# Layer 0 of a four-layer convolution stack: PSUM as one tile, four-bank results, copies of 768 columns

## The chip, the cores and the metric

The kernel runs on one core of a Trainium2 chip. Its time is the device time of one execution in microseconds (us), as a median over runs. A profile of one further execution shows what each engine did: TensorE (PE, with its weight loads, PEld), VectorE (DVE), ScalarE (ACT), GpSimd (POOL), and SyncE (SP), which issues DMAs.

## The reference, cut to what matters

The input is x with 4 images of 64 channels of 256 x 256, float32. Four layers follow one another; each adds to x a function of the group-normalised x. Only layer 0 is touched by the change:

```python
x = jnp.einsum('bchw,oc->bohw', x, w_in)            # 64 -> 384 channels, per pixel
xf = jnp.fft.rfft2(patches of 8 x 8) * fft_filter   # per channel, then back
x = depthwise 3 x 3 convolution of that
x1, x2 = jnp.split(x, 2, axis=1)
x = jax.nn.gelu(x1, approximate=False) * x2
return jnp.einsum('bchw,oc->bohw', x, w_out)        # 192 -> 64 channels
```

The filter on a patch and the depthwise convolution together are one linear map from the 64 pixels of a patch (and its neighbours) to 64 pixels, one for each of the 384 channels. Layer 1 is a 3 x 3 convolution, layer 2 a masked choice between two 1 x 1 convolutions, layer 3 a product in the Fourier domain.

## The kernel before, in words

Layer 0 cuts each image into rows of patches (32 rows, 32 patches each) and takes them in blocks of 11 rows: three blocks an image, 12 in all. For each block it loops four times (`kb`) over 48 channels of each kind, in two stages.

*Expansion* (`expand`, lines 459 to 490). One step takes half a normalised pair of patch rows from `xns`: 16 patches for each of two rows (index `s`; one row lies on partitions 0 to 63, the other on 64 to 127; at an image's edge the two halves hold the two halves of one row). The pixels are the stationary operand, `w_in` the moving one, so that a result has pixels of a patch on the partitions and channels along the columns. With `pairs` true (line 470) a stationary holds two neighbouring patches, 128 columns, and 16 matmuls make a step; otherwise (line 476) each patch is a stationary of its own and goes to the half of the partitions that suits the copies; that takes 32 matmuls. `pairs` is true for `kb` 0 and for the first six steps of the other passes (line 797).

The results of a step go to two PSUM tiles of two banks, one per `s`. PSUM is four such tiles, taken in turn by `banks` (line 278), for every purpose in layer 0. ScalarE copies the tile of `s` = 0 to the SBUF array `u`, VectorE that of `s` = 1: four copies each of 64 partitions x 384 columns when paired (line 486), three each otherwise (one of 128 partitions and two of 64; lines 488 to 490). `u` has a place for each patch of the block: on partitions 0 to 63 even patches at E1 and odd ones at O1, on partitions 64 to 127 odd ones at O2 and even ones at E2.

*Patch map* (`own` and `beside`, lines 514 to 550). For each group of two times two channels, 8 matmuls with the patch's own pixels (line 523) and 24 with those of its neighbours (line 539) accumulate in two tiles of `banks`; ScalarE takes the gelu of one bank (line 546), VectorE multiplies by the other (line 547), and POOL stores the result `h` to DRAM (line 550). Between groups, `unit` runs a part of the projection of the block before: `project` reads `g` back, multiplies by `w_out` (lines 632 and 639), and VectorE adds the result to x (lines 648 to 653).

The order on TensorE, VectorE, ScalarE and SP is as the code is written (`tc.manual_schedule`), so each engine goes through its instructions in program order. The framework sets the semaphores: it records which parts of which tiles an instruction reads and writes, and lets a later instruction wait for an earlier one that it conflicts with.

A block has 11 or 12 steps of expansion for each `kb` (`steps_of`, line 450): 32 stretches of 11 and 16 of 12, 544 steps in all.

Of the kernel before, what the change touches and what calls it, by code (L numbers as in the profile page):

```python
# [10 lines left out]
F32 = mybir.dt.float32  # L11
# [107 lines left out]
class _Net:  # L119
# [152 lines left out]
    def _layer0(self, ctx, dst):  # L272
        tc, nc, a, B, H, W = self.tc, self.nc, self.a, self.B, self.H, self.W
        pool = lambda name, bufs, **k: ctx.enter_context(tc.tile_pool(name=name, bufs=bufs, **k))
        pp = pool("l0p", 1, space=PSUM)
        turn = count()

        def banks(name):

            return pp.tile([128, 2, 512], F32, tag=f"p{next(turn) % 4}", name=name)  # L280

        self.small = lambda name: banks(name)[:, 0, :]
        P = PATCH
# [3 lines left out]
        CW = 2 * HC  # L287
# [3 lines left out]
        PB = HID // 4  # L291
        NR = 11
        L = CW * NR
        NG = PB // 4
        halves = [slice(0, C), slice(C, 128)]
# [121 lines left out]
        def load_x(part, p_x=p_x):  # L417
            b, i, k = part
            x0[part] = t = p_x.tile([128, 4, W], F32, tag="x", name=f"x0_{b}_{i}_{k}")
            for s in range(2):  # L420
                if k < 2:
                    nc.sync.dma_start(t[halves[s]], a["x"][b, :, P * (i + s) + 4 * k : P * (i + s) + 4 * k + 4, :])
                else:
                    nc.sync.dma_start(
                        t[halves[s]].rearrange("p r w -> p (r w)").rearrange("p (r w) -> p r w", r=P),
                        a["x"][b, :, P * i : P * i + P, s * HW2 : (s + 1) * HW2],
                    )

        def normalize_x(part, pool=False):
            b, i, k = part  # L430
            x = x0.pop(part).rearrange("p r w -> p (r w)")
            if k == 2:
                xns[b, i] = p_x1.tile([128, HW2 // P, P, P], F32, tag="x1", name=f"xn_{b}_{i}")
            elif k == 0:
                xns[b, i] = p_xn.tile([128, W // P, P, P], F32, tag="xn", name=f"xn_{b}_{i}")
            to = xns[b, i].rearrange("p m r w -> p r m w")
            if k < 2:
                to = to[:, 4 * k : 4 * k + 4]
            x = x.rearrange("p (r m w) -> p r m w", r=P if k == 2 else 4, w=P)
            if pool:  # L440
                nc.gpsimd.tensor_scalar(to, x, self.r[0][:, b : b + 1], self.nb[0][:, b : b + 1], ALU.mult, ALU.add)
            else:
                self.normalize(to, x, 0, b)
# [4 lines left out]
        E1, O1, O2, E2 = 0, HC, 1, HC  # L448

        def steps_of(p):  # L450

            b, i0 = blocks[p]
            one = lambda t: [(b, i0 + t, 0, [(t, 0), (t, 1)])] if 0 <= i0 + t < NP else []
            out = one(0)
            for t in range(1, NR, 2):
                out += [(b, i0 + t, q, [(t, q), (t + 1, q)]) for q in range(2)]
            return out + one(NR)

        def expand(p, kb, step, pairs):

            b, i, q, to = step
            ps = [banks(f"psu_{p}_{kb}_{i}_{q}_{s}") for s in range(2)]
            xn = xns[b, i][:, 16 * q : 16 * q + 16]
            lo, hi = halves
            for k in range(2):
                for m in range(4):
                    n, at = 2 * (4 * k + m), slice(2 * PB * m, 2 * PB * (m + 1))
                    for s in range(2):
                        if pairs:
                            nc.tensor.matmul(  # L470
                                ps[s][:, k, at], xn[halves[s], n : n + 2].rearrange("p n r w -> p (n r w)"),
                                win[halves[s], kb, 0 : 2 * PB], start=True, stop=True,
                            )
                            continue
                        for odd in range(2):
                            nc.tensor.matmul(  # L476
                                ps[s][halves[1 - odd], k, at], xn[halves[s], n + odd].rearrange("p r w -> p (r w)"),
                                win[halves[s], kb, PB * (1 - odd) : PB * (3 - odd)], start=True, stop=True,
                            )
            at = lambda h, o: u[h, :, o : o + 8].rearrange("p c (s m) -> p c s m", s=2)  # L480
            for s, copy in enumerate((nc.scalar.copy, nc.vector.tensor_copy)):
                o0 = to[s][0] * CW + 8 * to[s][1]
                v = ps[s][:, :, 0 : 8 * PB].rearrange("p s (m c) -> p c s m", m=4)
                if pairs:
                    for h, o, k, c in ((lo, O1, lo, 0), (hi, O2, lo, PB), (lo, E1 + 1, hi, 0), (hi, E2 + 1, hi, PB)):
                        copy(at(h, o0 + o), v[k, c : c + PB])  # L486
                    continue
                copy(at(slice(0, 128), o0 + 1), v[:, 0:PB])
                copy(at(hi, o0 + E2 + 1), v[lo, PB:])
                copy(at(lo, o0 + O1), v[hi, PB:])  # L490

        def load_w(j):

# [110 lines left out]
        def load_half(p, r, half):  # L604
            if 0 <= p < NB and r < P:
                if half == 0 and (p, r) not in rts:
                    load_r(p, r)
                load_g(p, r, half)
# [73 lines left out]
        with ordered:  # L682
# [38 lines left out]
            u = None  # L721
            ctx_u = ExitStack()
            u = ctx_u.enter_context(tc.tile_pool(name="l0u", bufs=1))
            u = u.tile([128, PB, (NR + 1) * CW + 2], F32, name="u")
            sources = []
            rows_u = u[:, :, 0 : (NR + 1) * CW].rearrange("p c (t w) -> p c t w", w=CW)
            lo, hi = halves
# [9 lines left out]
            for p in range(NB + 1):  # L737
# [24 lines left out]
                b, i0 = blocks[p]  # L762
                fresh = parts_of(p + 1) if p + 1 < NB else []
                steps = steps_of(p)
# [6 lines left out]
                def load_next(kb):  # L771
                    if kb == 3:
                        load_rows(2)
                    elif nk:
                        loaded.append(nk.pop(0))
                        load_stats(b + 1, loaded[-1])
# [10 lines left out]
                for kb in range(4):  # L787
                    for t in range(NR + 1):
                        if p == 0 and kb == 0:
                            if t == 1:  # L790
                                for part in first_parts[len(kept) :]:
                                    load_x(part)
                            for n in range(4) if t == 0 else range(t + 3, t + 4):
                                if n < len(first_parts):
                                    normalize_x(first_parts[n], pool=n % 2 == 1)
                        if t < len(steps):
                            expand(p, kb, steps[t], kb == 0 or t < (NR + 1) // 2)
                        if t in (0, 4) and first:
                            load_half(*first.pop(0))
                        if t == NR:  # L800
                            load_w(p * (HID // 8) + NG * kb // 2 + 3)
                            load_next(kb)
                    if p == 0 and kb == 0:
                        clear_sides()
                        ctx_f.close()
                        p_1, p_6 = (pool(n, 2, side="right") for n in ("l0g1", "l0g6"))
                        sources.append([p_1, p_6, pool("l0r", 2, side="right")])
                    for g in range(0, NG, 2):
                        if g > 0:
                            load_w(p * (HID // 8) + (NG * kb + g) // 2 + 3)  # L810
                        if g in (0, 2, 6, 8):
                            unit()
                        if g < 6 and kb < 3:
                            load_next(kb)
                        if kb == 3 and g == 0:
                            assert not self.norms
                            normalize_rows(3)
                        for k in range(2):
                            own(p, kb, g + k)
                        for k in range(2):  # L820
                            beside(p, kb, g + k)
                        if g < NG - 2 or kb == 2:
                            self.next_norms()
                        if kb == 3:
                            normalize_rows(2)
                            if p == NB - 1 and g < 2 * (NR // 2):
                                load_r(p, g // 2)
                            continue
                        if loaded:
                            next_stats(b + 1, loaded.pop(0))  # L830
                        if kb == 2 and g == NG - 2:
                            load_rows(2)
# [730 lines left out]
```

## Time and profile before

| | |
|---|---|
| median of 3 runs | 6347.42 us (6346.17 to 6354.44) |
| the profiled execution | 6345.01 us, span 6343.0 us |
| mean granted TensorE clock | 0.960 |
| PE busy | 5965.4 us (94% of the span) |
| weight loads | 3328.8 us (52%) |
| DVE busy | 4315.4 us (68%) |
| ACT busy | 3274.7 us (52%) |
| POOL busy | 1054.2 us (17%) |
| layer 0 | from the start to about 3790 us |

Busy times are sums over the whole span, so they mix stages with different limits; a line of a cost group gives the source line, engine, operation, what it writes and reads with shapes, the count, busy time and mean length of one, and then the engine's idle time just before those instructions with what ended it. Line numbers are those of the kernel before.

### The profile page before, as it was taken

The numbers are of one execution on the slowest core, as the hardware profiler recorded it, in microseconds if no ns is written. First come the engines' busy times: TensorE is split into PE (matmuls) and PEld (weight loads), VectorE is DVE, ScalarE is ACT, GpSimd is POOL, SyncE is SP. The second block draws the span as 40 slices with busy tenths as digits, with TensorE's granted clock in tenths as the row PEclk, the third lists the DMA queues.
The fourth block names the chain that finished last, engine by engine and source line by source line (L and its number), as shares of the span: only waits on it lengthen the run. The fifth ranks groups of instructions, "written<-read, shape, count | busy, mean of one in ns | idle before, by whom it ended". The sixth has DMA issues, their size and how long they took to land.

```text
span 6343.0 us, 233229 instructions
## 1 busy us (share of the span) xinstructions
PE 5965.4 (94%) x104150; PEld 3328.8 (52%) x104150; DVE 4315.4 (68%) x6003; ACT 3274.7 (52%) x4639; POOL 1054.2 (17%) x1651
## 2 busy tenths in 40 slices
PE   3999999999999999999999969999899999999987
PEld 2565655566665655556665533333344444443566
DVE  6566666666666666656665549999788988984265
ACT  4454444445454444344544407777777777772111
POOL 4111111111111111111111111111122222221011
PEclk9999999999999999999999979999999999999755
DMA  7477888887887878887768799999566666678799
GB/s 221 157 209 220 241 240 248 244 235 228 239 234 225 239 231 241 235 249 207 219 200 224 217 239 246 227 230 225 136 175 174 175 173 176 175 189 292 290 374 393
DMA packets 769595, 1441.98 MB, mean 227 GB/s; under 512 B 77412, under 2 KB 463476, under 8 KB 766548
## 3 DMA queue, kind: packets, MB, share of 16 engines
q1 hardware_dynamic: 616388, 917.72, 54.7%
q0 software_dynamic: 148672, 500.14, 23.5%
q8 instruction: 823, 13.48, 0.9%
q10 hardware_dynamic: 3536, 9.20, 0.6%
q14 instruction: 176, 1.44, 0.1%
HBM read 926.71 MB, written 500.04 MB: 225 GB/s over the span
## 4 chain that ended last, share of the span: by engine, by line
PE 83%; DVE 6%; DMA 6%; ACT 3%; issue 2%; POOL 0%; SPq 0%; ACTq 0%; POOLq 0%; DVEq 0%
PE pc L539 18%; PE pc L523 12%; PE m L946 10%; PE one L1187 9%; PE psu L470 8%; PE div L1146 7%; PE po L632 4%; DVE u L486 4%; PE psu L476 3%; PE psz L1176 2%; PE po L639 2%; ACT u L486 2%; PE psy L1521 2%; PE psa L1374 2%; DMA x<-x 2%
## 5 line engine op out<-in xcount | busy, mean ns | idle before, releaser
L547 DVE TENSOR_TENSOR h<-h,pc 128x374 f32<-128x374 f32 x1152 | 575.4, 541 | 1168.8 <-ACT h L546 1168.8
L546 ACT ACTIVATE h<-pc 128x374 f32<-128x374 f32 x1152 | 493.4, 480 | 1682.3 <-PE pc L539 1682.3
L539 PE MATMUL pc<-u,w 64*16 64x374 f32 (+2 forms) x27648 | 1178.0, 479 | 4.7 <-issue 4.5
L550 POOL DMA_DIRECT2D g<-h x576 | 415.5, 721 | 2834.5 <-DVE h L547 2724.2
L523 PE MATMUL pc<-u,w 64*64 64x374 f32 x9216 | 832.0, 484 | 10.1 <-DVE u L490 3.4
L486 DVE COPY u<-psu 64x384 f32<-64x384 f32 x1408 | 782.3, 556 | 60.4 <-PE psu L470 36.4
L539 PEld LDWEIGHTS pc<-u,w 64*16 64x16 f32 (+2 forms) x27648 | 465.5, 92 | 682.0 <-issue 645.4
L470 PE MATMUL psu<-win,xn 64*128 64x96 f32 x11264 | 759.9, 277 | 47.7 <-ACT u L486 26.7
L486 ACT COPY u<-psu 64x384 f32<-64x384 f32 x1408 | 722.8, 513 | 128.2 <-PE psu L470 100.8
L470 PEld LDWEIGHTS psu<-win,xn 64*128 64x128 f32 x11264 | 714.4, 188 | 114.3 <-ACT u L486 36.2
L1132 DVE TENSOR_TENSOR q<-xn 128x2313 f32<-128x2313 f32 (+2 forms) x256 | 628.0, 2495 | 1.7 <-ACT xn L253 1.7
L1187 PE MATMUL one<-z,wp 32*32 32x512 f32 x16384 | 598.1, 598 | 18.7 <-issue 14.9
L253 ACT ACTIVATE xn<-x,nb,r 128x1024 f32<-128x1024 f32 (+3 forms) x267 | 475.3, 1802 | 179.2 <-DMA x<-r 117.8
L523 PEld LDWEIGHTS pc<-u,w 64*64 64x64 f32 x9216 | 363.9, 132 | 383.5 <-issue 159.1
L1133 ACT ACTIVATE q<-q 128x2313 f32<-128x2313 f32 (+2 forms) x256 | 529.2, 2087 | 31.4 <-DVE q L1132 30.3
L1187 PEld LDWEIGHTS one<-z,wp 32*32 32x32 f32 x16384 | 368.7, 103 | 228.2 <-issue 87.7
L1146 PE MATMUL div<-q,ones 64*32 64x512 f32 x8192 | 465.9, 596 | 11.1 <-ACT q L1133 9.5
L1220 POOL DMA_DIRECT2D x<-r x512 | 274.5, 544 | 974.7 <-DVE r L1217 959.5
L476 PE MATMUL psu<-win,xn 64*64 64x96 f32 x12288 | 345.6, 250 | 39.9 <-issue 18.4
L632 PE MATMUL po<-g,wo 128*64 128x176 f32 (+1 forms) x3072 | 315.2, 348 | 45.0 <-DMA g<-g 36.9
L476 PEld LDWEIGHTS psu<-win,xn 64*64 64x64 f32 x12288 | 299.8, 135 | 82.3 <-issue 34.5
L946 PE MATMUL m<-t,wk 64*64 64x512 f32 x3072 | 341.1, 588 | 0.0
(157 smaller groups left out, 6428.7 us busy)
## 6 DMA issues: line engine op xcount, KB each, us to landing
g<-h POOLq DMA_DIRECT2D x576, 374.0 KB, 6.7
x<-x SPq DMA_DIRECT2D x240, 640.0 KB, 6.5
w<-wt SPq DMA_DIRECT2D x288, 448.0 KB, 6.9
x<-x SPq DMA_DIRECT2D x100, 1024.0 KB, 14.1
g<-g SPq DMA_DIRECT2D x414, 187.0 KB, 6.4
g<-g SPq DMA_DIRECT2D x736, 93.5 KB, 6.0
x<-in_x_dram SPq DMA_DIRECT2D x256, 256.0 KB, 8.0
x<-o POOLq DMA_DIRECT2D x128, 512.0 KB, 8.3
```

What stands on the lines that cost most here:

```text
L470: nc.tensor.matmul(ps[s][:, k, at], xn[halves[s], n : n + 2].rearrange("p n r w -> p (n r w)"), win[halves[s], kb, 0 : 2 * PB], start=True ...
L476: nc.tensor.matmul(ps[s][halves[1 - odd], k, at], xn[halves[s], n + odd].rearrange("p r w -> p (r w)"), win[halves[s], kb, PB * (1 - odd) ...
L486: copy(at(h, o0 + o), v[k, c : c + PB])
L523: nc.tensor.matmul(out(C * c, C, k, h), w[halves[h], k, 2 * (G % 2) + c, 0:C], cells(h, 4 * g + 2 * k + c, 0, 0), start=True, stop=False, ...
L539: nc.tensor.matmul(out(q, m, k, h), w[halves[h], k, 2 * (G % 2) + c, c0 : c0 + m], cells(h, 4 * g + 2 * k + c, down, right), start=False, ...
L547: nc.vector.tensor_mul(h[:, k], h[:, k], ps[k][:, 1, 0:L])
L632: nc.tensor.matmul(out(k, s, x), wo1, moving(g1[:, 2 * k], 2 * half + k, s, x), start=(x == 0), stop=False, skip_group_check=True,)
L946: nc.tensor.matmul(rows2(m)[halves[j], s], w[dx][halves[s]], ts[n][halves[s], i, 2 * j : 2 * j + 2, dx : dx + W], start=(dx == 0), stop=(d ...
L1132: nc.vector.tensor_sub(d, p0, p1)
L1133: nc.scalar.activation(d, d, AF.Square)
L1146: ins = nc.tensor.matmul(ps[quarters[j], h], ones[halves[h]], q[n, g, k][halves[h], r + 2 * j : r + 2 * j + 2, o : o + W], start=(m == 0), ...
L1187: ins = nc.tensor.matmul(rows2(ps[g])[quarters[j], k], w[quarters[i]], z[quarters[i], h, 2 * j + dy : 2 * j + dy + 2, dx : dx + W], tile_p ...
```

## The change: what it does

Only layer 0 is edited. PSUM becomes a single tile of 8 banks, and `banks` cuts `n` banks from it in turn, starting at a multiple of `n`; two for the old uses, four for an expansion step. The matmuls of a step write the four banks with the results of 8 patch pairs per `s` at one distance (128 columns, in place of 96 with a gap at the end of each bank), so that one access pattern covers both `s`. A copy then takes both `s` at once, 768 columns: ScalarE makes the two copies whose source is partitions 0 to 63, VectorE the two whose source is partitions 64 to 127. The target of a copy has two runs of 8 columns for each channel, at `o0` and `o1`. The call passes `True`, so that all steps take two patches per stationary; the branch for one patch stays in the code and isn't called.

```diff
-        turn = count()
-        def banks(name):
-            return pp.tile([128, 2, 512], F32, tag=f"p{next(turn) % 4}", name=name)
+        psum = pp.tile([128, 8, 512], F32, name="psum0")
+        turn = [0]
+        def banks(name, n=2):
+            k = -(-turn[0] // n) * n % 8
+            turn[0] = k + n
+            return psum[:, k : k + n]
...
-            ps = [banks(f"psu_{p}_{kb}_{i}_{q}_{s}") for s in range(2)]
+            ps = banks(f"psu_{p}_{kb}_{i}_{q}", 4)
...
-                    n, at = 2 * (4 * k + m), slice(2 * PB * m, 2 * PB * (m + 1))
+                    n, at = 2 * (4 * k + m), slice(128 * m, 128 * m + 2 * PB)
...
-                                ps[s][:, k, at], xn[halves[s], n : n + 2].rearrange("p n r w -> p (n r w)"),
+                                ps[:, 2 * s + k, at], xn[halves[s], n : n + 2].rearrange("p n r w -> p (n r w)"),
...
-            at = lambda h, o: u[h, :, o : o + 8].rearrange("p c (s m) -> p c s m", s=2)
-            for s, copy in enumerate((nc.scalar.copy, nc.vector.tensor_copy)):
-                o0 = to[s][0] * CW + 8 * to[s][1]
-                v = ps[s][:, :, 0 : 8 * PB].rearrange("p s (m c) -> p c s m", m=4)
-                if pairs:
-                    for h, o, k, c in ((lo, O1, lo, 0), (hi, O2, lo, PB), (lo, E1 + 1, hi, 0), (hi, E2 + 1, hi, PB)):
-                        copy(at(h, o0 + o), v[k, c : c + PB])
-                    continue
...
+            o0, o1 = (CW * t + 8 * s for t, s in to)
+            v = ps.rearrange("p b n -> p (b n)").rearrange("p (s m c) -> p c s m", s=2, m=8)
+            def copy(engine, h, o, k, c):
+                d = u[h]
+                d = bass.AP(tensor=d.tensor, offset=d.offset + o0 + o, ap=[d.ap[0], d.ap[1], [o1 - o0, 2], [1, 8]])
+                engine(d, v[k, c : c + PB])
+            act, dve = nc.scalar.copy, nc.vector.tensor_copy
+            if pairs:
+                copy(act, lo, O1, lo, 0)
+                copy(dve, lo, E1 + 1, hi, 0)
+                copy(act, hi, O2, lo, PB)
+                copy(dve, hi, E2 + 1, hi, PB)
...
-                            expand(p, kb, steps[t], kb == 0 or t < (NR + 1) // 2)
+                            expand(p, kb, steps[t], True)
```

More of the change, by code (lines that the diff above doesn't have):

```diff
@@ L476, in expand @@
                             nc.tensor.matmul(
-                                ps[s][halves[1 - odd], k, at], xn[halves[s], n + odd].rearrange("p r w -> p (r w)"),
+                                ps[halves[1 - odd], 2 * s + k, at], xn[halves[s], n + odd].rearrange("p r w -> p (r w)"),
                                 win[halves[s], kb, PB * (1 - odd) : PB * (3 - odd)], start=True, stop=True,
                             )
-            at = lambda h, o: u[h, :, o : o + 8].rearrange("p c (s m) -> p c s m", s=2)
-            for s, copy in enumerate((nc.scalar.copy, nc.vector.tensor_copy)):
-                o0 = to[s][0] * CW + 8 * to[s][1]
-                v = ps[s][:, :, 0 : 8 * PB].rearrange("p s (m c) -> p c s m", m=4)
-                if pairs:
-                    for h, o, k, c in ((lo, O1, lo, 0), (hi, O2, lo, PB), (lo, E1 + 1, hi, 0), (hi, E2 + 1, hi, PB)):
-                        copy(at(h, o0 + o), v[k, c : c + PB])
-                    continue
-                copy(at(slice(0, 128), o0 + 1), v[:, 0:PB])
-                copy(at(hi, o0 + E2 + 1), v[lo, PB:])
-                copy(at(lo, o0 + O1), v[hi, PB:])
+            o0, o1 = (CW * t + 8 * s for t, s in to)
[10 more added lines that the diff above has]
+                copy(dve, hi, E2 + 1, hi, PB)
+            else:
+                copy(act, slice(0, 128), 1, slice(0, 128), 0)
+                copy(dve, lo, O1, hi, PB)
+                copy(act, hi, E2 + 1, lo, PB)
         def load_w(j):
```

## The prediction

> **What bounds the kernel now.** I read the page's busy shares first, then the chain that ended last, the cost groups, the timeline of one expansion stretch engine by engine, and last the sums by stretch.
>
> The chain that ended last is TensorE's for the most part, with VectorE and ScalarE holding it for some 570 us:
>
> ```profile
> PE 83%; DVE 6%; DMA 6%; ACT 3%; issue 2%; POOL 0%; SPq 0%; ACTq 0%; POOLq 0%; DVEq 0%
> ```
>
> The page's cost groups give the work that the change touches:
>
> ```profile
> L486 DVE COPY u<-psu 64x384 f32<-64x384 f32 x1408 | 782.3, 556 | 60.4 <-PE psu L470 36.4
> ...
> L470 PE MATMUL psu<-win,xn 64*128 64x96 f32 x11264 | 759.9, 277 | 47.7 <-ACT u L486 26.7
> L486 ACT COPY u<-psu 64x384 f32<-64x384 f32 x1408 | 722.8, 513 | 128.2 <-PE psu L470 100.8
> ...
> L476 PE MATMUL psu<-win,xn 64*64 64x96 f32 x12288 | 345.6, 250 | 39.9 <-issue 18.4
> ```
>
> 1408 copies by four are 352 expansion steps with two patches per stationary; lines 488 to 490 have 192 copies each on each engine, so 192 more steps with one patch: 544 steps. L470 has 11264 records, two for each of 16 matmuls of a step.
>
> The timeline of TensorE, then ScalarE, then VectorE at the start of a stretch (start, length, instruction, count, idle time before it and what ended it):
>
> ```profile
> 452.81 3.81 PE L470 MATMUL psu<-win,xn 64*128 64x96 f32 x64
> 457.10 5.16 PE L470 MATMUL psu<-win,xn 64*128 64x96 f32 x68 [0.48 <-ACT u L486]
> ```
> ```profile
> 454.92 6.43 ACT L486 COPY u<-psu 64x384 f32<-64x384 f32 x12 [1.13 <-PE psu L470]
> 461.51 2.12 ACT L486 COPY u<-psu 64x384 f32<-64x384 f32 x4 [0.16 <-PE psu L470]
> 463.81 2.12 ACT L486 COPY u<-psu 64x384 f32<-64x384 f32 x4 [0.17 <-PE psu L470]
> ```
> ```profile
> 454.91 13.74 DVE L486 COPY u<-psu 64x384 f32<-64x384 f32 x24 [0.46 <-PE psu L470]
> ```
>
> TensorE needs 3.81/2 = 1.9 us for a step and 2.1 us from its first matmul to the first copy (452.81 to 454.92). VectorE runs 24 copies without a gap: 573 ns each, 2.29 us a step. ScalarE keeps that rhythm with idle time in it, and TensorE is let go by a copy. So a paired step is set by four VectorE copies, side by side with four of ScalarE's. A step of one patch has three copies per engine, about 1.73 us.
>
> The sums of the expansion stretch and of the stretch after it:
>
> ```profile
> 452.80:479.50 26.70, 25.57 (x619) 23.11 (x615) 24.35 (x44) 22.43 (x44) 1.41 (x2) 1.00 0.39 104
> 479.50:528.00 48.50, 48.34 (x869) 21.41 (x860) 24.18 (x42) 9.41 (x22) 10.07 (x14) 1.00 1.00 295
> ```
>
> (PE, weight loads, DVE, ACT, POOL busy; clock; DMA share, GB/s.) In the first VectorE and ScalarE are nearly full and the DMA engines are not. The second is TensorE's: 48.34 of 48.50 us. There are 48 such stretches. From the first expansion matmul to the first matmul of line 523 they take 1283.5 us in all by the timeline, 26.7 us each. Everything outside them belongs to other work.
>
> [...] The changed copies split the partitions (ScalarE reads 0 to 63, VectorE 64 to 127), [...] the 3.40 us from 599.0 have a clock of 0.50.
>
> **The change, part by part.** The decisive part is not in the copies but in their waits. PSUM is now one tile with banks cut out of it, and the copies of both engines read all four banks of a step. The built program of the changed kernel names what each waits for (ScalarE two steps, then VectorE ten):
>
> ```
> L489 TensorCopy u<-psum_90 64x48x2x8 [waits PE_49,Activation_49]
> L489 TensorCopy u<-psum_90 64x48x2x8 [waits DVE_49]
> L489 TensorCopy u<-psum_90 64x48x2x8 [waits PE_49,Activation_49]
> L489 TensorCopy u<-psum_90 64x48x2x8 [waits DVE_49]
> L489 TensorCopy u<-psum_90 64x48x2x8 [waits Activation_49] x20
> ```
>
> By their values: VectorE's first copy waits for ScalarE's first, ScalarE's second for VectorE's first, VectorE's second for ScalarE's second, in all 544 steps. Before, a VectorE copy waited for TensorE alone. The framework evidently treats two instructions on one bank of one tile as a conflict, whatever their partitions. The first matmul of a step waits for VectorE's last copy of the step before last, which had the same four banks.
>
> Copy lengths. VectorE: 556 ns for 384 columns; add 384 at 1.04 ns (the slope from 374 columns, 541 ns, to 1032 columns, 1226 ns, on lines 547 and 936): 0.96 us. Bounds: [...] 1.11 (twice 556). ScalarE: line 486 shows 481/522/533 ns as least, median and most; only one of the four targets, the even one (E2+1), has the short time, and both ScalarE copies now go to odd ones (O1, O2). Line 1180's 1024 columns take 1033 ns, so 0.81 ns a column: 482 + 312, and the 40 ns of an odd target twice, since runs of 8 double: 0.875 us; bounds 0.79 and 1.04. Handoffs, medians of idle times in this trace: ACT to DVE 33 ns (line 546 to 547), DVE to ACT 93 (1132 to 1133), DVE to PE 54 (547 to 523; up to 290).
>
> One pair of steps on one half of PSUM: 2.05 (matmuls to first copy) + 0.875 + 0.033 + 0.96 + 0.093 + 0.875 + 0.033 + 0.96 + 0.054 = 5.93 us. The two halves alternate, so 2.97 us a step. The engines alone would give almost the same: the next step's first ScalarE copy runs beside VectorE's last, so 2 x 0.96 + 0.875 + 0.13 = 2.92. The half's own loop is the longer one and sets it.
>
> A stretch: step 0 ends at 2.05 + 3.83 = 5.88; step 1 at 5.89 + 0.96 + 0.093 + 0.875 + 0.033 + 0.96 = 8.81; then 5.93 per two steps. 11 steps: 5.88 + 5 x 5.93 = 35.5, with release 35.6; 12 steps: 8.81 + 29.65 + 0.05 = 38.5. There are 32 stretches of 11 and 16 of 12 steps: 1139 + 616 = 1755 us, against 1283.5: **+472 us**.
>
> The rest. All rows paired: 192 steps get 16 matmuls in place of 32, but with stationaries of 128 columns; their 1.9 us lie under the 2.97 us, so nothing is won; if the waits were gone, 1.9 to 2.05 us would be the step. Half the copy instructions save about 4 x 0.16 us of fixed time a step, which is inside the sum. Rotation of banks: 4 units and 12 results of two pairs of banks bring it back to a multiple of four, so no extra bank is skipped in the steady order. Lines 523, 546 and 547 now wait by bank rather than by tile; that stage is TensorE's with little idle time (10.1 us for line 523 in all), so zero, at worst 20 us. What queues behind: on ScalarE the next step's first copy stands behind the copy that waits for VectorE; on VectorE the projection's add (line 648) behind the last copy, 1.4 us, needed only about 1.9 us after the stretch ends. The projection's matmuls (2.5 us), which now cover a tail of about 2 us after the expansion, must wait for the half before last, but still end ahead of the last copy, so they cost nothing more. Loads and stores (SP, POOL) keep their order and get more time; line 632's idle time for g (36.9 us) lies almost wholly after the last stretch, so none comes back.
>
> Against the profiled execution: 6345.0 (span 6343.0) + 472 = 6817; the median of the runs is 2.4 us higher: **6820 us**.
>
> **Rivals.**
> *The copies run together after all* (the waits cost nothing, or aren't what they seem). Then a step takes 2 x 0.96 on VectorE, and a half's loop 2.05 + 1.95 + 0.05 = 4.05 for two, 2.03 a step: 4.0 + 10 x 2.03 = 24.3 and 26.3 us, 1198 in all, so -85 and 6262 us. It decides where a step comes under about 2.2 us, (26.7 - 2.05)/11.3. For it speaks only that the partitions are apart; against it, that 544 steps carry the waits.
> *The clock falls as well.* TensorE would be busy 1.95 of 2.97 us, 66%. In the first stretch before, the changed rhythm is met: 4.33 of 6.80 us busy (126.2 to 133.0) at a clock of 1.00. That speaks against it, [...]. At half clock a half's loop grows by 1.95, a step by 0.98: a third of the steps gives +177, 7000 us; all, +530, 7350.
> *The chain is a little shorter or longer.* [...] With 0.29 for DVE to PE, and 50 ns more on each copy, 6.37: +115, 6935.
>
> **Chances.** Main case with its bounds, 6735 to 6935: 0.78. Clock falling, 6935 to 7350: 0.14. Slower, but by less than 390 us (waits partly hidden): 0.04. Together faster: 0.03. No change: 0.01. A change within 0.2% (13 us) is about what a measurement of this kernel can't tell from none. Range 6735 to 6980: the main case and the nearer third of the clock's.
>
> **What would show it.** Right: copies of 768 columns at about 0.96 (DVE) and 0.88 us (ACT); VectorE's copies idle before each until ScalarE's, ScalarE's second until VectorE's, together some hundreds of us that were 60 and 128; steps 2.97 us apart, TensorE idle about 1 us before each; the stretches after still 48 us; POOL, layers 1 to 3 unchanged. Wrong: both engines' copies overlapping, steps near 2 us, or a clock under 0.9 in the expansion stretches.

## The result and the profile after

The changed kernel takes 6942.66 us (median of 4 runs, 6922.36 to 6949.53), the kernel before 6348.66 us beside it: a ratio of 1.0933, 95% interval 1.0919 to 1.0948. The profiled execution took 6943.21 us with a span of 6941.1 us, 598 us more than before, and the mean granted TensorE clock went from 0.960 to 0.918.

The page of the changed kernel: the clock row (40 slices of the span, tenths of full speed), the chain that ended last, and the cost groups of the expansion (count, busy us and mean ns of one, then the engine's idle time before it and what ended it):

```profile
PEclk9988988988899899899988998899999999999855
...
PE 75%; DVE 9%; ACT 8%; DMA 5%; issue 2%; SPq 0%; POOL 0%; ACTq 0%; POOLq 0%; DVEq 0%
...
L473 PE MATMUL psum<-win,xn 64*128 64x96 f32 x17408 | 1351.9, 319 | 385.5 <-DVE u L489 373.6
L489 DVE COPY u<-psum 64x768 f32<-64x768 f32 x1088 | 1044.5, 960 | 795.8 <-ACT u L489 787.1
...
L489 ACT COPY u<-psum 64x768 f32<-64x768 f32 x1088 | 956.7, 879 | 865.2 <-DVE u L489 565.1
```

The copies of an engine are 1088, two a step, as long as foreseen. In front of them VectorE sits idle for 787 us until ScalarE's copy and ScalarE for 565 us until VectorE's; on the chain that ended last the two now hold 17% of the span, 9% before. TensorE's matmuls (L473) wait 373.6 us for the last copy. But they also take 319 ns each, where the paired ones took 277 before: that is the clock, as e11 below shows (277 ns again, with 6.8 us at half clock).

The timeline of the start of one stretch that kept the full clock: TensorE, then ScalarE, then VectorE (start, length, instruction, count, idle time before it and what ended it):

```profile
774.93 2.25 PE L473 MATMUL psum<-win,xn 64*128 64x96 f32 x34
777.34 2.02 PE L473 MATMUL psum<-win,xn 64*128 64x96 f32 x30 [0.17 <-issue]
780.76 2.03 PE L473 MATMUL psum<-win,xn 64*128 64x96 f32 x32 [1.40 <-DVE u L489]
783.67 2.03 PE L473 MATMUL psum<-win,xn 64*128 64x96 f32 x32 [0.88 <-DVE u L489]
786.74 0.47 PE L473 MATMUL psum<-win,xn 64*128 64x96 f32 x4 [1.04 <-DVE u L489]
```
```profile
777.00 0.84 ACT L489 COPY u<-psum 64x768 f32<-64x768 f32 x1 [1.10 <-PE psum L473]
778.87 1.75 ACT L489 COPY u<-psum 64x768 f32<-64x768 f32 x2 [1.03 <-DVE u L489]
```
```profile
777.88 0.96 DVE L489 COPY u<-psum 64x768 f32<-64x768 f32 x1 [1.32 <-ACT u L489]
779.75 1.95 DVE L489 COPY u<-psum 64x768 f32<-64x768 f32 x2 [0.91 <-ACT u L489]
```

One reads the chain off the starts: ScalarE 777.00, VectorE 777.88, ScalarE 778.87, VectorE 779.75, each some 0.03 us after the other engine's copy ended; when VectorE's second is done, TensorE starts at 780.76 on the same half of PSUM, and again at 786.74. A half's loop is 5.98 us, 2.99 a step.

And the start of a stretch that lost the full clock, TensorE alone:

```profile
603.08 3.81 PE L473 MATMUL psum<-win,xn 64*128 64x96 f32 x64
608.91 7.03 PE L473 MATMUL psum<-win,xn 64*128 64x96 f32 x64 [2.02 <-DVE u L489]
616.59 1.58 PE L473 MATMUL psum<-win,xn 64*128 64x96 f32 x24 [0.65 <-DVE u L489]
```

Two steps take 3.81 us at first and 7.03 us after the pause.

The sums of three stretches (PE, weight loads, DVE, ACT, POOL busy with counts; clock; DMA share, GB/s):

```profile
346.00:383.60 37.60, 36.26 (x296) 31.04 (x298) 18.24 (x19) 18.97 (x22) 0.00 (x0) 0.50 0.08 24
...
689.98:727.79 37.81, 26.66 (x425) 24.30 (x421) 23.33 (x26) 22.17 (x27) 1.41 (x2) 1.00 0.45 121
774.93:809.87 34.94, 24.82 (x391) 22.40 (x385) 21.16 (x23) 20.23 (x24) 2.82 (x3) 1.00 0.64 155
```

The last two are whole stretches at full clock: 34.94 us for 11 steps and 37.81 for 12. The first is a time at half clock that begins in a stretch and ends in the patch map after it; stretches of 12 steps that lost the clock in this way take up to 47 us. By the timeline the 48 stretches take 1870.0 us in place of 1283.5: +586.5 of the 598. During them 626.8 us are at half clock, 13.7 before. Of the other 12 us, 3 lie between the stretches and 8 behind the last one. (Between them the first matmuls of line 533 after each stretch take 162.0 us in all, 139.5 before, with 8.1 us at half clock; other parts there got shorter.)

### The profile page after: what moved, and what is told of

Its sections match the earlier page's. It is cut to its first block, busy times and chain, and to the rows that moved or that the text cites. A ratio compares the mean times of both kernels' runs of the same rounds, so it can differ in the third digit from the quotient of the medians.

```text
span 6941.1 us, 218922 instructions
## 1 busy us (share of the span) xinstructions
PE 6238.6 (90%) x98006; PEld 3622.2 (52%) x98006; DVE 4256.0 (61%) x5107; ACT 3213.5 (46%) x3743; POOL 1053.9 (15%) x1651
## 4 chain that ended last, share of the span: by engine, by line
PE 75%; DVE 9%; ACT 8%; DMA 5%; issue 2%; SPq 0%; POOL 0%; ACTq 0%; POOLq 0%; DVEq 0%
PE psum L549 16%; PE psum L533 11%; PE psum L473 10%; PE m L956 10%; DVE u L489 8%; PE one L1197 8%; ACT u L489 7%; PE div L1156 6%; PE psum L642 4%; PE psz L1186 2%; PE psum L649 2%; DMA x<-x 2%; PE psa L1384 2%; PE psy L1531 1%; PE zero L1197 1%
## 5 line engine op out<-in xcount | busy, mean ns | idle before, releaser
L473 PE MATMUL psum<-win,xn 64*128 64x96 f32 x17408 | 1351.9, 319 | 385.5 <-DVE u L489 373.6
L489 DVE COPY u<-psum 64x768 f32<-64x768 f32 x1088 | 1044.5, 960 | 795.8 <-ACT u L489 787.1
L473 PEld LDWEIGHTS psum<-win,xn 64*128 64x128 f32 x17408 | 1271.0, 229 | 486.5 <-DVE u L489 440.6
L489 ACT COPY u<-psum 64x768 f32<-64x768 f32 x1088 | 956.7, 879 | 865.2 <-DVE u L489 565.1
L557 DVE TENSOR_TENSOR h<-h,psum 128x374 f32<-128x374 f32 x1152 | 574.7, 541 | 1148.8 <-ACT h L556 1148.8
L556 ACT ACTIVATE h<-psum 128x374 f32<-128x374 f32 x1152 | 493.1, 480 | 1685.0 <-PE psum L549 1684.9
L549 PE MATMUL psum<-u,w 64*16 64x374 f32 (+2 forms) x27648 | 1176.0, 479 | 0.8 <-issue 0.8
L533 PE MATMUL psum<-u,w 64*64 64x374 f32 x9216 | 844.0, 485 | 11.6 <-DVE u L489 7.0
L549 PEld LDWEIGHTS psum<-u,w 64*16 64x16 f32 (+2 forms) x27648 | 465.3, 92 | 675.6 <-issue 633.3
L533 PEld LDWEIGHTS psum<-u,w 64*64 64x64 f32 x9216 | 391.0, 133 | 371.4 <-issue 197.2
```

The costliest lines, as they stand in the source:

```text
L473: nc.tensor.matmul(ps[:, 2 * s + k, at], xn[halves[s], n : n + 2].rearrange("p n r w -> p (n r w)"), win[halves[s], kb, 0 : 2 * PB], start ...
L489: engine(d, v[k, c : c + PB])
L533: nc.tensor.matmul(out(C * c, C, k, h), w[halves[h], k, 2 * (G % 2) + c, 0:C], cells(h, 4 * g + 2 * k + c, 0, 0), start=True, stop=False, ...
L549: nc.tensor.matmul(out(q, m, k, h), w[halves[h], k, 2 * (G % 2) + c, c0 : c0 + m], cells(h, 4 * g + 2 * k + c, down, right), start=False, ...
L556: nc.scalar.activation(h[:, k], ps[k][:, 0, 0:L], AF.Gelu)
L557: nc.vector.tensor_mul(h[:, k], h[:, k], ps[k][:, 1, 0:L])
```

## The experiments

Each was timed on one chip together with the kernel before, which took 6340.01 to 6348.66 us there; a ratio is to that. "Stretches" is the sum of the 48 expansion stretches in the one trace of that kernel; e1 and e10, the same kernel twice, differ by 3 us in it.

| kernel | us | ratio, 95% interval | stretches, us | of it at half clock |
|---|---|---|---|---|
| before | 6348.66 | 1 | 1283.5 | 13.7 |
| the changed kernel | 6942.66 | 1.0933 (1.0919 to 1.0948) | 1870.0 | 626.8 |
| e1, no waits between the copies | 6300.35 | 0.9933 (0.9917 to 0.995) | 1249.9 | 0 |
| e2, copies split by s | 6388.96 | 1.0074 (1.0059 to 1.0089) | 1330.5 | 0 |
| e3, other order of the copies | 6941.84 | 1.0949 (1.0915 to 1.0984) | 1886.3 | 569.2 |
| e4, before with all rows paired | 6409.29 | 1.0108 (1.0089 to 1.0127) | 1336.5 | 0 |
| e5, half the matmuls done twice | 7050.22 | 1.1118 (1.11 to 1.1136) | 1952.4 | 0 |
| e6, two stationaries a pair | 6859.12 | 1.0816 (1.0797 to 1.0836) | 1764.0 | 262.5 |
| e7, e6 without the waits | 6501.65 | 1.025 (1.0231 to 1.027) | 1465.6 | 273.1 |
| e8, before with no row paired | 6466.13 | 1.0191 (1.017 to 1.0212) | 1412.9 | 273.1 |
| e9, e1 with part of the rows unpaired | 6290.42 | 0.992 (0.9906 to 0.9934) | 1246.4 | 13.7 |
| e10, e1 again | 6298.56 | 0.9931 (0.9917 to 0.9945) | 1252.9 | 0 |
| e11, doubled in the second step alone | 6788.51 | 1.0705 (1.0689 to 1.0721) | 1724.5 | 6.8 |
| e12, doubled in all but the first two | 7066.52 | 1.1143 (1.1121 to 1.1165) | 1970.1 | 150.2 |

The theory at the outset: the waits between the copies of a step, which the framework sets because all four banks belong to both engines' copies, serialise them. Rivals: that the wide copies themselves or the pairing of all rows cost the time, or that the engines' strict turns do, whatever the banks.

### e1: the waits alone taken out

```diff
-                engine(d, v[k, c : c + PB])
+                return engine(d, v[k, c : c + PB]).ins
...
-                copy(act, lo, O1, lo, 0)
-                copy(dve, lo, E1 + 1, hi, 0)
-                copy(act, hi, O2, lo, PB)
-                copy(dve, hi, E2 + 1, hi, PB)
+                a1 = copy(act, lo, O1, lo, 0)
+                d1 = copy(dve, lo, E1 + 1, hi, 0)
+                a2 = copy(act, hi, O2, lo, PB)
+                d2 = copy(dve, hi, E2 + 1, hi, PB)
+                for x, y in ((d1, a1), (a2, d1), (d2, a1), (d2, a2)):
+                    tc.declare_no_dep(x, y, reason="other partitions of the banks")
```

> The changed kernel with one thing taken out: the framework is told that a step's copies of ScalarE (partitions 0 to 63) and of VectorE (64 to 127) don't depend on each other, so each waits for TensorE alone. Copies, matmuls and banks stay. Theory (the waits between the copies cost the time, and the clock fell because TensorE had to wait): steps of about 2.03 us, stretches of 24.3 and 26.3 us, 6262 us, clock near 1.00 in the expansion. Rival (the two engines can't read one bank together, or the copies, the single PSUM tile or the paired rows cost it): above 6700 us.

6300.35 us, 0.7% faster than the kernel before. The cost groups of its page:

```profile
L473 PE MATMUL psum<-win,xn 64*128 64x96 f32 x17408 | 1082.8, 276 | 75.4 <-DVE u L489 56.9
L489 DVE COPY u<-psum 64x768 f32<-64x768 f32 x1088 | 1044.5, 960 | 131.2 <-PE psum L473 113.4
```

And the start of a stretch in its timeline, ScalarE's and VectorE's copies:

```profile
670.78 3.59 ACT L489 COPY u<-psum 64x768 f32<-64x768 f32 x4 [1.10 <-PE psum L473]
```
```profile
670.78 3.90 DVE L489 COPY u<-psum 64x768 f32<-64x768 f32 x4 [0.45 <-PE psum L473]
```

Both engines start at 670.78 and run four copies side by side, out of the same banks; VectorE's 960 ns are unchanged, and its 787 us of waiting for ScalarE are gone. So the waits, and nothing in the wide copies, serialise the step.

The gain over the kernel before is smaller than the rival "run together" gave (6262). Its stretches of 11 steps take 22.97 us where no projection is in them and 25.28 us where one is. VectorE waits 113 us for TensorE: with 16 matmuls of 128 columns a step, TensorE's 2.0 us are as long as VectorE's 1.92, so it seems that nothing covers the projection's 2.3 us any more; no run took the projection away.

### e2 and e4: wide copies and pairing apart

e2 keeps one PSUM tile, four banks and pairing, and lets each engine copy its own two banks as before:

```diff
-            v = ps.rearrange("p b n -> p (b n)").rearrange("p (s m c) -> p c s m", s=2, m=8)
...
+            for s, copy in enumerate((nc.scalar.copy, nc.vector.tensor_copy)):
+                o0 = CW * to[s][0] + 8 * to[s][1]
+                v = ps[:, 2 * s : 2 * s + 2].rearrange("p s (m c) -> p c s m", m=4)
+                for h, o, k, c in ((lo, O1, lo, 0), (hi, O2, lo, PB), (lo, E1 + 1, hi, 0), (hi, E2 + 1, hi, PB)):
+                    copy(at(h, o0 + o), v[k, c : c + PB])
```

> The changed kernel (one PSUM tile, four banks at one stride, all rows paired), with the copies shared out as before: ScalarE takes the two banks of s = 0, VectorE those of s = 1, four copies of 384 columns each, no bank read by both. Theory of the waits: no engine waits for the other, a step is VectorE's 4 x 0.573 = 2.29 us, stretches of 27.1 and 29.3 us, 6400 us. Rival (the single tile, or pairing all rows, is what costs): above 6800 us.

e4 is the kernel before with the pairing alone:

```diff
-                            expand(p, kb, steps[t], kb == 0 or t < (NR + 1) // 2)
+                            expand(p, kb, steps[t], True)
```

> The kernel before with one part of the change alone: all rows with two patches per stationary; PSUM tiles and copies as before. 192 steps go from three copies per engine (about 1.75 us) to four (2.29 us): +0.54 x 192 = +104 us at most, about +55 by the sums of paired stretches (27.1 and 29.3 against 25.4 and 27.2 for mixed ones): 6400 to 6450 us. If pairing is what costs the change its time: above 6800 us.

Their stretches agree: 27.03 and 29.11 us in e2, 27.09 and 29.18 in e4. So PSUM as one tile costs nothing by itself, and pairing all rows costs about 1%: +53 us over the stretches of before, since those 192 steps now have four VectorE copies in place of three.

### e3: the copies in another order

```diff
                 copy(act, lo, O1, lo, 0)
-                copy(dve, lo, E1 + 1, hi, 0)
                 copy(act, hi, O2, lo, PB)
+                copy(dve, lo, E1 + 1, hi, 0)
                 copy(dve, hi, E2 + 1, hi, PB)
```

> The changed kernel with the four copies of a step in another order: both of ScalarE, then both of VectorE, so one handover between engines a step in place of three. The engines' own chain falls to 1.93 us a step. Theory (the loop of one half of PSUM sets the step: 2.05 + 2 x 0.88 + 0.03 + 2 x 0.96 + 0.05 = 5.81 us for two steps): 2.9 us a step as before at full clock, 6900 us or, as TensorE's idle time now comes in one piece of 1.9 us, more by a clock at half. Rival (the alternation of the engines sets the step): 1.93 to 2.05 us a step, about 6270 us.

6941.84 us, the changed kernel's time. The one stretch of 12 steps that kept the full clock takes 38.04 us, against 37.8:

```profile
2783.75:2821.79 38.04, 26.55 (x425) 24.59 (x421) 23.38 (x26) 23.23 (x28) 1.44 (x2) 1.00 0.41 115
```

With ScalarE's two copies first, the engines hand over once a step and not three times, and the next step's copies can overlap more; the four copies on one set of banks remain in a row, and VectorE still sits idle for 763.5 us until ScalarE's copies. It is this loop of matmuls and four copies on one half of PSUM that sets the step, as the prediction had it, and not the engines' taking turns.

### e5: TensorE given more to do

```diff
-            for k in range(2):
+            for k in (0, 1, 1):
```

The matmuls of k = 1 write the same results a second time.

> The changed kernel with TensorE given more work in the expansion: half of a step's matmuls (8 of 16, those of k = 1) are done twice, with the same result. It measures the clock's part. At full clock a half's loop grows by 0.97 us, a step by 0.49, 544 steps by 265 us. Theory (the array's clock fell because TensorE idled too much between steps): TensorE is busy 2.9 of 3.5 us, the clock stays at 1.00, the 147 us of the clock are won back, 7060 us. Rival (the clock falls with the rhythm of waits or the copies, not with the idle share): clock as low as in the changed kernel, 7200 us or more.

7050.22 us and no half clock at all in the stretches: most take 39.4 to 39.5 us with 11 steps and 43.18 with 12. The clock row of its page:

```profile
PEclk9999999999999999999999999799999999999955
```

Half as many matmuls again cost 108 us: the loop of a half is longer by the added 0.95 us, which is 0.48 a step or some 260 us in 544 steps, and part of that is given back with the clock. In the stretch of 12 steps from 703.74 TensorE was busy for 37.13 of 43.48 us, in the changed kernel's from 689.98, which kept the full clock, for 26.66 of 37.81. With 626.8 us of half clock gone for this filling, the half clock comes from TensorE's idle time, though this run doesn't say from which. From it alone I took the steady rhythm (busy two thirds of the time) for the cause; e11 and e12 showed otherwise.

### e6 to e8: stationaries of 64 columns

Could shorter weight loads (135 ns on average for 64 columns, line 476 of the kernel before, 188 for 128, line 470) make up for the waits, or replace the pairing? e6 gives each patch its own stationary in the changed kernel:

```diff
-                            nc.tensor.matmul(
-                                ps[:, 2 * s + k, at], xn[halves[s], n : n + 2].rearrange("p n r w -> p (n r w)"),
-                                win[halves[s], kb, 0 : 2 * PB], start=True, stop=True,
-                            )
+                            for odd in range(2):
+                                nc.tensor.matmul(
+                                    ps[halves[odd], 2 * s + k, at], xn[halves[s], n + odd].rearrange("p r w -> p (r w)"),
+                                    win[halves[s], kb, 0 : 2 * PB], start=True, stop=True,
+                                )
```

> The changed kernel with the same results and copies, but each pair of patches loaded as two stationaries of 64 columns (32 matmuls a step, each to one half of the partitions). TensorE then needs about 1.75 us a step (124 records of line 476 took 3.40 us in the kernel before; a step has 64) against 1.95. Theory: at full clock the loop of a half is 5.6 us, the engines' chain 2.92 a step sets it: stretches 0.5 us shorter; but TensorE idles more, so the clock is at half at least as often: 6900 to 7050 us. Rival (pairing patches is what costs): below 6800 us.

e7 is the same edit on e1, and e8 the kernel before with `False` passed to `expand`, so that no row is paired.

> Both together: the copies without waits between the engines, and two stationaries of 64 columns in place of one of 128. In the run without those waits TensorE (1.95 us) and VectorE (1.92) were nearly level and the projection's 2.3 us after the expansion showed again (stretches of 25.28 us where it follows, 22.97 where not). With TensorE at 1.75, VectorE sets the step at 1.95 and the projection hides under the last copies: stretches of about 24.3 and 26.2, 6255 us. Rival (VectorE was the limit anyway): 6300 us.

> The kernel before, the other way round from the change: all rows with one patch per stationary, PSUM tiles and copies as before. A step has three copies per engine, 1.73 us on VectorE, and 1.75 us on TensorE: stretches of about 22.4 and 24.2 us against 25.4 to 29.2, 6165 us. Rival (TensorE becomes the limit or its clock falls): 6340 us or more.

None came out as its theory had it. e6 lies between its two forecasts: a step's matmuls take 1.55 us in place of 2.03, which shortens the loop (33.8 and 36.5 us a stretch at full clock), and there was less half clock than in the changed kernel although TensorE is busy for less. e7 and e8 were slower by far. The rival of e8 had named a fall of the clock, which came, but none had foreseen what is seen in front of it. TensorE in e8, a part of one stretch:

```profile
621.60 5.39 PE L476 MATMUL psu<-win,xn 64*64 64x96 f32 x126 [3.67 <-issue]
629.33 2.37 PE L476 MATMUL psu<-win,xn 64*64 64x96 f32 x101 [2.34 <-issue]
632.01 0.96 PE L476 MATMUL psu<-win,xn 64*64 64x96 f32 x25 [0.32 <-ACT u L490]
633.41 2.37 PE L476 MATMUL psu<-win,xn 64*64 64x96 f32 x103 [0.44 <-issue]
636.19 0.88 PE L476 MATMUL psu<-win,xn 64*64 64x96 f32 x23 [0.40 <-ACT u L490]
637.50 2.44 PE L476 MATMUL psu<-win,xn 64*64 64x96 f32 x105 [0.43 <-issue]
```

The pauses marked "issue" wait for nothing that the profile shows, and they come after 126 matmul records each time (126, 101 + 25, 103 + 23), with as many weight loads: every 252 instructions. In all, issue pauses before line 476 come to 259.4 us in e8, 18.4 in the kernel before; in e7 they are 232.5, in e6, where the waits spread the same matmuls over more time, 62.7. The page's queue for instructions fits: from the kernel before to e8 it has 88 packets and 1.45 MB more for 21804 more instructions, 16.5 KB a packet and 66 bytes an instruction, about 250 instructions a packet. From this I estimate that TensorE used up the short matmuls here faster than their instructions arrived. It is read from the spacing (elsewhere in e8 the pauses come at the same distance or at two or three times it); no run changed the supply of instructions alone. Nor do the runs tell the cost of the pauses from that of the clock, which fell in 46 of e8's 48 stretches and in 45 of e7's, 273.1 us at half clock in each.

### e9 and e10: the fastest version

e9 is e1, in which the steps that before took one patch per stationary take two stationaries of 64 columns again:

```diff
+                        if half:
+                            for odd in range(2):
+                                nc.tensor.matmul(
+                                    ps[halves[odd], 2 * s + k, at], xn[halves[s], n + odd].rearrange("p r w -> p (r w)"),
+                                    win[halves[s], kb, 0 : 2 * PB], start=True, stop=True,
+                                )
+                            continue
...
-                            expand(p, kb, steps[t], True)
+                            expand(p, kb, steps[t], True, kb > 0 and t >= (NR + 1) // 2)
```

> The copies of a step run together, and the steps in the second half of the expansion rows, in the blocks after an image's first, where only the part before took one patch per stationary, use two stationaries of 64 columns again; all other steps keep one of 128. If TensorE at about 2.0 us a step is what holds the version with the copies run together, the one-patch steps give back up to a microsecond in each of the stretches that hold a projection: about 6260 to 6290 us. If one-patch matmuls also bring their pauses of 'issue' back, some 18 us of them as in the kernel before, nothing is left of the gain: 6295 to 6315. If the clock falls as in the versions with halves everywhere, above 6320.

> The version with the copies of a step run together once more, beside the mixed one on the same chip: 6300 us, 0.993 of the kernel before, if the gain of 0.7% is there in every job; within 0.2% of the kernel before if it was that job's own.

On one chip: 6290.42 us (0.992, 0.9906 to 0.9934) and 6298.56 (0.9931, 0.9917 to 0.9945). Both beat the kernel before by about 0.7 to 0.8%, and e1's gain is there a second time; the two can't be told apart. e9's smooth stretches are shorter (24.67 against 25.28 us), and its issue pauses of 19.9 us before the short matmuls, with four falls of the clock, seem to take most of that back.

### e11 and e12: which idle time drops the clock

In the changed kernel's trace the clock falls in 36 stretches, for the first time always 5.4 to 8 us after their start. All 36 began like the stretch at 603.08 above: 64 matmul records without a break, then 2.01 to 2.11 us of idle time until the first half of PSUM is free. (In ten of them the clock fell inside this pause, 1.58 to 1.97 us after it began.) The four stretches in which TensorE chanced to stop earlier, so that this pause was 0.65 to 1.40 us (774.93 above), kept the full clock; so did eight of the 44 with the long one. The trace of e3 says the same: the clock fell in 47 of its stretches, and the one that escaped, 2783.75 above, is again one in which TensorE stopped early, with pauses of 0.72 and 1.02 us; where it paused for 1.59 or 1.65 us there, the clock fell. e11 fills the pause and leaves the steady rhythm as it is; e12 does the reverse.

```diff
-            for k in range(2):
+            for k in (0, 1, 1) if more else (0, 1):
...
-                            expand(p, kb, steps[t], True)
+                            expand(p, kb, steps[t], True, t == 1)
```

e12 has `t > 1` in that place; both repeat matmuls with the same results.

> The changed kernel, in which only the second step of each stretch does the matmuls of k = 1 twice (the same results once more). In its trace the clock fell in 36 of 48 stretches, always 5.4 to 8 us after the stretch began, and only where TensorE had paused 2.01 to 2.11 us in one piece between the second step and the third; the four stretches with a pause of 0.65 to 1.40 us kept the full clock through the same steady rhythm. The extra 0.95 us lies in that pause and shortens it to about 1.1. If the pause at the start is what drops the clock: next to no time at half clock, stretches of 35.0 and 37.8 to 38 us throughout, 1725 us in all in place of 1870, and about 6800 us, 1.071 of the kernel before. If the steady rhythm does it (TensorE busy two thirds of the time): half clock as in the changed kernel, and 6920 to 6950 us.

> The other way round: the matmuls of k = 1 are done twice in all steps but the first two of a stretch, so that the pause of 2.0 us at its start stays and the later rhythm is as busy as with the doubling everywhere. If the pause at the start drops the clock: half clock again in about 36 stretches, from 5 to 8 us on, some 200 us of it or far more, as a filled step needs 5.7 us at half clock, and a time above the 7050 us of the doubling everywhere, 7100 to 7500. If the steady rhythm does it: no half clock, and about 7040 us.

e11: 6788.51 us, 154 us less than the changed kernel (some 146 by the ratios) for 16 more matmul records in each of 48 steps. Its clock row, its matmul group, and one whole stretch of 12 steps at the start:

```profile
PEclk9999999999999999999999997999999999999855
...
L473 PE MATMUL psum<-win,xn 64*128 64x96 f32 x18176 | 1141.5, 277 | 448.2 <-DVE u L489 439.6
```
```profile
670.29 4.71 PE L473 MATMUL psum<-win,xn 64*128 64x96 f32 x80
676.13 2.03 PE L473 MATMUL psum<-win,xn 64*128 64x96 f32 x32 [1.13 <-DVE u L489]
```

The matmul is back at 277 ns, the pause is 1.13 us here and at most 1.22 in the other stretches with the full clock, and TensorE is idle for longer than before the edit (448 us in front of these matmuls, 385 in the changed kernel): the steady two thirds do not drop the clock. One fall is left, in the very first stretch, 11.4 us after its start and behind a pause of 1.83 us. In e12 the pause is there again (2.0 to 2.15 us in one piece, in three stretches 1.6 to 1.7), and so is the fall, in 33 stretches, 5.4 to 8 us from the start:

```profile
433.13 3.81 PE L473 MATMUL psum<-win,xn 64*128 64x96 f32 x64
439.03 7.20 PE L473 MATMUL psum<-win,xn 64*128 64x96 f32 x70 [2.08 <-DVE u L489]
```

Its time, 7066.52 us, lies under the 7100 to 7500 that this theory gave: the half clock lasts only 3.4 or 6.8 us each time, where the changed kernel had 13 stretches with some 24 us of it or more. Its sum of stretches is 18 us above e5's; about 43 us come off for two unfilled steps (38.5 against 39.4 us a stretch), so the falls cost some 61 us. e11 and e12 together settle where the fall comes from: the pause at the start of a stretch. Its length alone is not shown to be what counts: e11 also makes the run of matmuls ahead of it longer, 4.71 us for 3.81.

What also stays open is how long the clock stays down. In the changed kernel some falls ended after 6.8 us, others lasted 34 us and more, though TensorE was then busy for 36.26 of 37.60 us; no run varied that.

## Why the prediction was right

The time of 6942.66 us lies in the range, 123 us above the forecast. The mechanism of the main case was right, but its own bounds ended at 6935: it is the part of the clock's rival which the range took in that came true. There is some luck in it too, as the stretches without the clock were forecast 31 us too long; with that added the time would be 6974 us, and the range ends at 6980. The runs split the 586.5 us of the stretches into differences of their sums; the last two rows take e11 as the changed kernel at full clock, as its filling lies in a pause, and its stretches are mostly as long as those that kept the clock without it (34.9 to 35.0 and 37.8 us).

| step | from, to | us |
|---|---|---|
| pairing all rows | before, e4 | +53.0 |
| PSUM as one tile | e4, e2 | -6.0 |
| one copy over both s, the engines side by side | e2, e1 | -80.6 |
| waits between the copies | e1, e11 | +474.6 |
| half clock | e11, the changed kernel | +145.5 |

*The waits between the copies.* Right, and decisive: they are in the trace as 787 and 565 us, and e1 takes them away with all the loss.

*Copy lengths and handoffs.* 0.960 us on VectorE for 0.96 foreseen; on ScalarE a median of 0.882 for 0.875. Handoffs are 0.03 us both ways, where 0.093 was foreseen from VectorE to ScalarE.

*The loop of a half.* 5.98 us for 5.93, and e3 shows that it is what sets the step. The first release comes at 5.83 us for 5.88. The low end of the main case, 6735 us, was my estimate; no run bears on it.

*The stretches.* 35.6 and 38.5 us were foreseen, 34.95 and 37.8 measured at full clock; e11's sum is +441 where the forecast had +472. The fault is at the end: the prediction lets the patch map wait for the last copy. In the stretch from 774.93 the last VectorE copy runs from 809.92 to 810.88, 35.95 us after the start for 35.5 foreseen; but line 533's first matmuls start at 809.87, 1.0 us before the copy's end. The next ones do wait for it, to 810.94, so part of this comes back behind the stretches: line 533's first matmuls after each take 156.7 us in all in e11, 139.5 before.

*The rest at zero.* Right to 12 us of 598. That pairing would be free under the new step is not contradicted, as its 53 us are a cost only where the copies set the step; but the prediction did not see that it costs about 1% alone.

*The clock.* This is the term that was mis-sized: taken as nothing in the main case, it is 145.5 us. The rival "the clock falls as well", at 0.14, is what happened, in nearly the amount given for "a third of the steps" (+177): a third of the stretches' time, 626.8 of 1870.0 us, was at half clock. What failed is the argument against it, "TensorE would be busy 1.95 of 2.97 us, 66%", met before at a clock of 1.00 (4.33 of 6.80 us). About the steady rhythm this was true. But the working had the cause in its own numbers: two steps of matmuls need 3.81 us, the first half is free at 5.88, so TensorE stands still for 2.07 us at the start of each stretch. That gap was priced as time and not looked at for the clock. The trace of the kernel before had examples: in four of its stretches the clock fell within 0.8 us of the end of an "issue" pause of 3.09, 2.64, 2.09 or 1.10 us (they end at 2121.04, 2425.34, 3019.29 and 3318.59), and the fall at 599.0, which the prediction cites, came after one of 1.91 us, with TensorE busy for 1.49 of the 3.40 us ahead of it. In the changed kernel it fell at gaps of 2.01 to 2.11 us in 36 of 44 stretches and not in the other eight; no run shows what tells these apart.

*Copies run together.* Right that it would not happen, as the waits were there. Its 6262 us were too good by 38: e1 has TensorE at the same 2.0 us as VectorE and the projection in the open.

## What to carry to other kernels

Before engines share a PSUM tile, look at what the framework takes for a conflict: here it was the bank, whatever the partitions, and waits between copies that could run together cost 475 us, while the same copies without them beat both kernels (the one before by 0.7%). When a loop gets a new bound, look at its first turns as well as at its rhythm: two halves filled at once and then one long pause for the first to come free cost 146 us through the clock, and repeating a few matmuls in that pause gave nearly all of it back.

## What the runs showed of the hardware

- In the changed kernel a single TensorE pause of 2.01 to 2.11 us, between matmuls at full rate, was met by half clock, from 0.5 us before its end to 1.8 us after it, in 36 of 44 stretches, pauses of 0.65 to 1.40 us at that place in none of four. This is no threshold: in e3 pauses of 1.59 and 1.65 us were followed by falls, in the kernel before one of 1.10 us.
- In the changed kernel a rhythm of 2.03 us of matmuls in 2.99 us went with the full clock throughout in 12 of 48 stretches, and in e11 in 47 of 48; in e6 one stretch with 20.71 us of matmuls in 36.50 also kept it.
- Once down, the clock of the changed kernel stayed at half for 3.4 to 41 us. In one such time of 37.6 us TensorE was busy for 96% by its records.
- In e1 two engines copied from the same PSUM banks at the same time, on different partitions, with no change in VectorE's 960 ns (ScalarE: 887 ns on average for 879).
- In e8 streams of matmuls with 64-column stationaries stopped at a distance of 252 instructions, for 0.4 to 3.7 us in the stretch shown.
